# Four fused convolution layers: the order in which two engines empty the score tiles of layer 3, and the engine that normalises its input

## The chip, the cores and the metric

The kernel runs on one core of one Trainium2 chip. The metric is the device time of one execution in microseconds (us); lower is better. Five engines work side by side, each on its own queue of instructions in the order of the program: TensorE (in the profile PE for matmuls and PEld for its weight loads), VectorE (DVE), ScalarE (ACT), GpSimd (POOL) and SyncE (SP, which here only starts transfers). Matmuls write to PSUM, the accumulation memory; VectorE and ScalarE read it from there, GpSimd does not.

## The reference, cut to what matters

An input of 4 images, 256 channels, 48 x 48 points goes through four layers. Each adds its result to its input, and each starts by normalising the input in groups of 8 channels. Layer 3 is an attention whose sums run over square windows:

```python
def _gn(v, G=32, eps=1e-5):                 # group normalisation: (v - mean) / sqrt(var + eps)
    ...
def _L3_conv_ref(x, Wq, Wk, Wv, Wout, bout):        # WINDOWS = (1, 2, 4), HEADS = 8
    q = jax.nn.sigmoid(q)                   # q, k, v: projections of x, 8 heads of 32 channels
    k = jax.nn.sigmoid(k)
    v = v / jnp.maximum(jnp.linalg.norm(v, axis=1, keepdims=True), 1e-12)
    Ik = _integral(k)
    Ikv = _integral(jnp.einsum('bfhw,bghw->bfghw', k, v))
    for w in WINDOWS:
        ws = Hh // w                        # windows of 48, 24 and 12 points
        wk, wkv = _box(Ik, ws, Hh, Ww), _box(Ikv, ws, Hh, Ww)
        attn = jnp.einsum('bdhw,bdfhw->bfhw', q, wkv)
        norm = jnp.einsum('bdhw,bdhw->bhw', q, wk)
        outs.append((attn / (norm[:, None] + 1e-06)).reshape(b, C, Hh, Ww))
    return jnp.einsum('bchw,oc->bohw', jnp.concatenate(outs, axis=1), Wout) + bout[None, :, None, None]
...
x = x + _L3_conv_ref(_gn(x), L3_conv_Wq, L3_conv_Wk, L3_conv_Wv, L3_conv_Wout, L3_conv_bout)
```

For every query point this is: scores q.k against all key points, those outside the window set to zero, times v, for three windows.

## The kernel before

Layers 0 to 2 come first; towards their end the projections of the first image of layer 3 are woven in between them. The rest is the loop of layer 3. It walks over "tiles": one tile is a block of 128 keys (8 rows by 16 columns, block row `a`, block column `c` of 3) against a block of queries (8 rows, block row `rb`), for 4 heads. For the 4 images, two halves of the heads and six query blocks there are 720 tiles.

The four heads of a tile are two pairs. A pair's scores fill one PSUM tile `s` of two banks, one bank for each head, and there are two such tiles in all, so that the first pairs of all tiles share one and the second pairs the other:

```python
tc.tile_pool(name="smp", bufs=2 * (LAG + 1), reuse_waits="tile") as smp,      # LAG = 2
tc.tile_pool(name="ps_s", bufs=2, space=PSUM, reuse_waits="tile") as ps_s,
...
def scores(self, pr, a, c):
    s = ps_s.tile([P, 2, 512], F32, tag="s", name="s")
    for j in range(2):
        pe.matmul(s[:, j, ...], kvs[...][0][head, c, :], self.qs[head, r0:r1, c0:c1], start=True, stop=True)
```

Two engines empty `s` into the tiles `sm0`, `sm1`, `sm2` in SBUF, one for each window. `copy` (ScalarE) moves the columns on which the widest window has no edge, `widest` (VectorE) multiplies the columns beside them with a mask of zeros and ones, `middle` (VectorE) makes `sm1` by the mask of the middle window. GpSimd then makes `sm2` out of `sm0`:

```python
full = abs(a - rb) * RB + RB <= HALVES[0]      # all rows of the tile lie within the widest window
many = seen(NW - 1, a, rb)                     # the smallest window sees the tile: a "near" tile

def middle(s, tiles):
    if full and many:
        of_banks(s, tiles, 1, rows_seen(1, a, rb), cols_seen(1, c))       # dve.tensor_mul by mask 1
def copy(s, tiles):
    if full:
        act.copy(view(tiles, 0, (r0, r1), (f0, f1)), s[:, :, :, f0 - c0 : f1 - c0])
def widest(s, tiles):
    if not full:
        of_banks(s, tiles, 0, *all0)
        return
    for p0, p1 in ((c0, f0), (f1, c1)):
        if p0 < p1:
            of_banks(s, tiles, 0, (r0, r1), (p0, p1))                     # dve.tensor_mul by mask 0

first, second = zip(ss, pairs)
copy(*first)
middle(*second)
copy(*second)
middle(*first)
widest(*first)
widest(*second)
for tiles in pairs:
    wi = NW - 1 if many else 1
    if wi in wis:
        times_mask(pool, wi, ...)                                         # sm2 (or sm1) from sm0
```

TensorE runs two tiles behind with the sums: in one step it takes the scores of tile n, then the sums of tile n - 2 (`acc`, four heads for each window that sees the tile):

```python
for n in range(len(stream) + LAG):
    if n < len(stream):
        ss = [blocks[i].scores(pr, a, c) for pr in range(NPR)]
        ahead.append(blocks[i].masked(a, c, ss))
    if n >= LAG:
        sms = ahead.pop(0)
        for wi in (1, 0, 2):
            if wi in sms[0]:
                blocks[i].sums(wi, a, c, sms)
    advance()                      # one step of all jobs beside the loop: projections, norms, outputs
```

A query block alternates near tiles and the others ("far") as long as it has both. Tiles whose key rows are two blocks away are far but `full`; three blocks away they are not full, and VectorE empties them alone.

The projections of layer 3 take their input from `xn`, the normalised rows of x, made by VectorE with mean and reciprocal deviation from `st3`:

```python
xn = self.scr.tile([P, NCT, NKC, P], F32, tag="xn", name="xn")
for ct in range(NCT):
    dve.tensor_scalar(
        xn[:, ct].rearrange("p c (r x) -> p c r x", x=KC),
        xr[:, ct].rearrange("p r (c x) -> p c r x", x=KC),
        st3[:, b, 0, ct : ct + 1], st3[:, b, 1, ct : ct + 1], ALU.subtract, ALU.mult,
    )
    yield 1
...
# end of layer 2, once for each image
dve.tensor_copy(st3[:, b, 0, :], m3)
dve.tensor_copy(st3[:, b, 1, :], r3)
```

Of the kernel before, what the change touches and what calls it, by code (L numbers as in the profile page):

```python
# [15 lines left out]
AF = mybir.ActivationFunctionType  # L16
ALU = mybir.AluOpType
# [128 lines left out]
def conv_preact_kernel(  # L146
# [50 lines left out]
    st3 = const.tile([P, B, 2, NCT], F32, name="st3")  # L197


    pe, dve, act, pool, sync = (  # L200
        InOrder(tc, e) for e in (nc.tensor, nc.vector, nc.scalar, nc.gpsimd, nc.sync)
    )
# [69 lines left out]
    def take(what):  # L272
        while free[what] == 0:
            yield 1
        free[what] -= 1
# [11 lines left out]
    class Projection:  # L287
# [13 lines left out]
        def load(self, g, a, n):  # L301

            b = self.b
            yield from take("xr")
            if self.enough:
                free["xr"] += 1
                self.left.append(g)
                return
            xr = self.scr.tile([P, NCT, RB, W], F32, tag="xr", name="xr")
            sync.dma_start(  # L310
                out=xr,
                in_=x3_d[b][:, a * RB : (a + 1) * RB, :].rearrange(
                    "(ct p) r w -> p ct r w", p=P
                ),
            )
            yield FETCH
            yield from take("xn")
            xn = self.scr.tile([P, NCT, NKC, P], F32, tag="xn", name="xn")
            for ct in range(NCT):
                dve.tensor_scalar(  # L320
                    xn[:, ct].rearrange("p c (r x) -> p c r x", x=KC),
                    xr[:, ct].rearrange("p r (c x) -> p c r x", x=KC),
                    st3[:, b, 0, ct : ct + 1],
                    st3[:, b, 1, ct : ct + 1],
                    ALU.subtract,
                    ALU.mult,
                )
                yield 1
            free["xr"] += 1
            self.xn[g], self.uses[g] = xn, n  # L330
# [102 lines left out]
        def groups(self, groups):  # L433

            def load(n):
                a, names = groups[n]
                return self.load(n, a, sum(NKC if name == "v" else 1 for name in names))

            yield load(0)
            for n, (a, names) in enumerate(groups):
                if n + 1 < len(groups):
                    yield load(n + 1)
                for name in names:
                    if name == "v":
                        for c in range(NKC):
                            yield self.v(n, a, c)
                    else:
                        yield self.qk(n, a, name[0], int(name[1]))  # L450


    with (
# [766 lines left out]
        def layer2(b, stats):  # L1220
# [102 lines left out]
            late()  # L1323
            fill(1.5)
            m3, r3 = stats.end(fill)
            dve.tensor_copy(st3[:, b, 0, :], m3)
            dve.tensor_copy(st3[:, b, 1, :], r3)

        def prelude(b):
# [99 lines left out]
        with (  # L1429
# [11 lines left out]
            first = ExitStack()  # L1441
# [18 lines left out]
            for b in range(B):  # L1460
                if b + 1 < B:
                    filler = conv0(b + 1, {})
                else:
                    ending.close()
                    wts3 = ctx.enter_context(tc.tile_pool(name="wts_qkv", bufs=1, side="right"))
                    filler = project_first()
                    masks = wts3.tile([P, NMASK], BF16, name="masks")
                    nc.gpsimd.dma_start(out=masks, in_=masks_in[:, 0:NMASK])
                stats = attend(b)
                for _ in side:  # L1470
                    fill(1.5)
                load_wl1(0)
                load_wl1(1)
                load_wl2(0)
                layer2(b, layer1(b, stats))
                if b + 2 < B:
                    prelude(b + 2)
                else:
                    fill_all()
# [3 lines left out]
    with (  # L1483
# [187 lines left out]
        def rows_seen(wi, a, rb):  # L1671

            h = HALVES[wi]
            return (
                max(0, a * RB - h + 1 - rb * RB),
                min(RB, a * RB + RB + h - rb * RB),
            )

        def cols_seen(wi, c):
            h = HALVES[wi]  # L1680
            return max(0, c * KC - h + (wi > 0)), min(W, c * KC + KC + h)

        class Block:
# [28 lines left out]
            def masked(self, a, c, ss):  # L1712

                rb = self.rb
                all0 = rows_seen(0, a, rb), cols_seen(0, c)
                (r0, r1), (c0, c1) = all0
                wis = [wi for wi in range(NW) if seen(wi, a, rb)]
                pairs = [
                    {
                        wi: smp.tile(  # L1720
                            [P, 2, RB, min(W, KC + 2 * HALVES[wi])],
                            F32,
                            tag=f"sm{wi}",
                            name=f"sm{wi}",
                        )
                        for wi in wis
                    }
                    for _ in ss
                ]

                def view(tiles, wi, rows, cols):
                    (y0, _), (x0, _) = rows_seen(wi, a, rb), cols_seen(wi, c)
                    return tiles[wi][
                        :, :, rows[0] - y0 : rows[1] - y0, cols[0] - x0 : cols[1] - x0
                    ]

                def times_mask(engine, wi, rows, cols, dst, src):
                    mr = rb * RB + rows[0] - (a * RB - HALVES[wi] + 1)
                    mc = cols[0] - (c * KC - MCOL0[wi])
                    nr, ncol = rows[1] - rows[0], cols[1] - cols[0]  # L1740
                    m = mask[wi][:, mr : mr + nr, mc : mc + ncol]
                    engine.tensor_mul(
                        dst, src, m.unsqueeze(1).to_broadcast([P, 2, nr, ncol])
                    )

                def of_banks(s, tiles, wi, rows, cols):
                    src = s[:, :, rows[0] - r0 : rows[1] - r0, cols[0] - c0 : cols[1] - c0]
                    times_mask(dve, wi, rows, cols, view(tiles, wi, rows, cols), src)

                f0, f1 = max(0, c * KC + KC - HALVES[0]), min(W, c * KC + HALVES[0] + 1)
                full = abs(a - rb) * RB + RB <= HALVES[0]

                many = seen(NW - 1, a, rb)

                def middle(s, tiles):
                    if full and many:
                        of_banks(s, tiles, 1, rows_seen(1, a, rb), cols_seen(1, c))

                def copy(s, tiles):
                    if full:
                        act.copy(
                            view(tiles, 0, (r0, r1), (f0, f1)), s[:, :, :, f0 - c0 : f1 - c0]
# [8 lines that stand above are left out]
                            of_banks(s, tiles, 0, (r0, r1), (p0, p1))  # L1773

                first, second = zip(ss, pairs)
                copy(*first)
                middle(*second)
                copy(*second)  # L1780
                middle(*first)
                widest(*first)
                widest(*second)
                for tiles in pairs:

                    wi = NW - 1 if many else 1
                    if wi in wis:
                        rows, cols = rows_seen(wi, a, rb), cols_seen(wi, c)
                        src = view(tiles, 0, rows, cols)
                        times_mask(pool, wi, rows, cols, view(tiles, wi, rows, cols), src)  # L1790
                return [
                    {wi: view(t, wi, rows_seen(wi, a, rb), cols_seen(wi, c)) for wi in wis}
                    for t in pairs
                ]
# [28 lines left out]
        def seen(wi, a, rb):  # L1823
            r0, r1 = rows_seen(wi, a, rb)
            return r0 < r1
# [226 lines left out]
```

## Time and profile before

Three runs took 3774.7, 3778.4 and 3779.35 us, with a median of 3778.4 us. The profiled execution spans 3775.4 us.

| | whole span, 3775.4 us | loop of layer 3, 1440 to 3776 us |
|---|---|---|
| PE busy | 3264.8 | 2078.07 |
| PEld busy | 1879.4 | 941.82 |
| DVE busy | 2487.2 | 1543.65 |
| ACT busy | 1036.2 | 771.29 |
| POOL busy | 1518.1 | 1361.85 |

The first column is from the page's first part, the second is the sum of a table of busy time by stretch. The engines work side by side, so the rows don't add up. Matmuls overlap one another and their ends are modelled, so a busy PE isn't necessarily at its peak. Nearly every instruction is issued through one helper and carries its line number (L142); the groups are told apart by the names of their tiles, written out<-in: `sm<-s` empties a score tile, `acc<-sm,vs` are the sums. "idle before ... <-X" is the idle time of an engine just before such instructions, and what ended it.

### The profile page before, as it was taken

What the parts mean: (1) busy time and instruction counts of PE and PEld (TensorE: products, weight loads), DVE (VectorE), ACT (ScalarE), POOL (GpSimd) and SP (SyncE); (2) the same over time, 40 slices, a digit from 0 to 9 for tenths busy, and PEclk for the clock granted to TensorE, in tenths of its full rate; (3) what the DMA queues carried; (4) which work ended last, traced back from release to release, by engine and by line L of the source; (5) the groups of instructions that cost most, each with busy time, mean ns of one, the idle gap of its engine ahead of it and who ended that gap; (6) DMA issues with size and microseconds to landing.
All of it is one profiled execution on the core that took longest, in us unless ns stands there. A gap on an engine that the chain in (4) does not pass through costs nothing. (4 is left out here: it accounts for less than half of the span.)

```text
span 3775.4 us, 68847 instructions
## 1 busy us (share of the span) xinstructions
PE 3264.8 (86%) x26498; PEld 1879.4 (50%) x26498; DVE 2487.2 (66%) x5119; ACT 1036.2 (27%) x2025; POOL 1518.1 (40%) x2184
## 2 busy tenths in 40 slices
PE   3688898998996788988889889899899899989998
PEld 2467686786784564433334334344443344444443
DVE  7876587587583366777666567756577766556665
ACT  0012111111113322433222333332344332233331
POOL 0000120020020034778765486755365766344332
PEclk9798999999997899999999899999999999999999
DMA  7745323324324313345434243533223444101122
GB/s 250 238 135 170 100 104 116 109 95 125 109 75 124 102 70 108 125 136 159 125 103 131 90 136 122 164 97 108 78 95 123 139 116 116 47 31 53 41 60 60
DMA packets 373019, 423.04 MB, mean 112 GB/s; under 512 B 129076, under 2 KB 328532, under 8 KB 371540
## 3 DMA queue, kind: packets, MB, share of 16 engines
q1 hardware_dynamic: 371491, 416.32, 35.6%
q8 instruction: 211, 3.46, 0.4%
q0 software_dynamic: 144, 1.52, 0.2%
q14 instruction: 117, 0.95, 0.1%
q10 hardware_dynamic: 1056, 0.79, 0.1%
HBM read 288.79 MB, written 131.25 MB: 111 GB/s over the span
## 5 line engine op out<-in xcount | busy, mean ns | idle before, releaser
L142 DVE TENSOR_TENSOR sm<-s,masks 128x112 f32<-128x112 f32 (+10 forms) x2592 | 1135.8, 493 | 765.5 <-PE s L142 321.1
L142 POOL TENSOR_TENSOR sm<-sm,masks 128x432 f32<-128x432 f32 (+14 forms) x1152 | 853.3, 755 | 936.5 <-ACT sm L142 672.0
L142 PE MATMUL s<-qs,ks 32*128 32x320 f32 (+3 forms) x5760 | 832.5, 500 | 200.1 <-DVE sm L142 151.2
L142 ACT COPY sm<-s 128x528 f32<-128x528 f32 (+2 forms) x1152 | 594.9, 535 | 1470.7 <-PE s L142 1169.9
L142 PE MATMUL acc<-sm,vs 128*32 128x384 f32 (+18 forms) x13440 | 880.5, 385 | 16.1 <-POOL sm L142 15.8
L142 PEld LDWEIGHTS s<-qs,ks 32*128 32x128 f32 x5760 | 374.1, 185 | 604.7 <-DVE sm L142 232.8
L142 PE MATMUL cv<-vx,wt 128*128 128x288 f32 x2080 | 559.3, 425 | 90.7 <-DVE vx L142 49.1
L142 PEld LDWEIGHTS acc<-sm,vs 128*32 128x32 f32 x13440 | 355.2, 110 | 551.3 <-issue 348.6
L142 PEld LDWEIGHTS cv<-vx,wt 128*128 128x128 f32 x2080 | 402.4, 198 | 212.4 <-issue 53.6
L142 POOL MEMSET v<- 128x16 f32 (+1 forms) x120 | 18.6, 215 | 725.7 <-DVE vx L142 635.7
L142 PE MATMUL cv<-v,wl 128*128 128x384 f32 x1152 | 224.5, 354 | 24.4 <-DVE x L142 9.2
L142 PEld LDWEIGHTS cv<-v,wl 128*128 128x128 f32 x1152 | 214.8, 195 | 34.6 <-issue 16.1
L142 POOL TENSOR_TENSOR pt<-pt 128x144 f32<-128x144 f32 x336 | 187.4, 558 | 22.8 <-DVE pt L142 0.5
L142 POOL TENSOR_TENSOR v<-l2v,v 128x384 fp32r<-128x384 f32 x96 | 109.2, 1168 | 130.2 <-ACT v L142 121.4
L142 POOL TENSOR_TENSOR nhi<-nhi,nq 128x384 f32<-128x384 f32 x144 | 148.3, 1058 | 0.0
L142 PE MATMUL cv<-pad,wl 128*128 128x384 bf16 x864 | 143.1, 327 | 0.0
L142 PE MATMUL out_ps<-o,wout_sb 128*128 128x384 f32 x288 | 122.8, 509 | 9.4 <-DVE o L142 5.4
L142 PE MATMUL out_ps<-stage,wout_sb 128*128 128x384 f32 x288 | 117.3, 489 | 0.4 <-DVE stage L142 0.4
L142 PE MATMUL proj_ps<-wv_sb,xn 128*128 128x256 f32 x288 | 89.5, 438 | 32.3 <-ACT vt L142 19.1
L142 DVE TENSOR_TENSOR vx<-v 128x868 f32<-128x868 f32 x112 | 115.4, 1056 | 0.5
L142 PE MATMUL ap<-seen,xT 120*128 120x120 f32 (+3 forms) x832 | 113.5, 293 | 0.0
L142 PEld LDWEIGHTS <-wl 128*128 128x128 bf16 x864 | 83.8, 97 | 59.1 <-issue 0.4
(162 smaller groups left out, 2859.0 us busy)
## 6 DMA issues: line engine op xcount, KB each, us to landing
wt<-wt SPq DMA_DIRECT2D x48, 768.0 KB
kb_d<-pt SPq DMA_DIRECT2D x48, 576.0 KB
rc<-r_d SPq DMA_DIRECT2D x192, 144.0 KB
nhi<-kb_d SPq DMA_DIRECT2D x120, 192.0 KB
nlo<-kb_d SPq DMA_DIRECT2D x88, 192.0 KB
o_d<-stage SPq DMA_DIRECT2D x24, 576.0 KB
o<-o_d SPq DMA_DIRECT2D x24, 576.0 KB
wl<-wl_d SPq DMA_DIRECT2D x16, 768.0 KB
```

The source lines that it names most:

```text
L142: return lambda *args, **kwargs: self.tc.keep_in_program_order(op(*args, **kwargs))
```

## The change

For near tiles (`full and many`) the order is another: VectorE empties the first pair (`middle`, then `widest`) while ScalarE copies the second pair; then they change over, ScalarE copies the first pair and VectorE does the second. The other tiles keep their order. It is meant to let VectorE begin with the pair that is ready first, and to have each of the two score tiles emptied in one go. Separately the normalisation of the rows of x moves from VectorE to ScalarE, as an activation x * r + (-m * r); `st3` therefore holds -m * r in place of m.

```diff
@@ -317,13 +317,12 @@
             for ct in range(NCT):
-                dve.tensor_scalar(
+                act.activation(
                     xn[:, ct].rearrange("p c (r x) -> p c r x", x=KC),
                     xr[:, ct].rearrange("p r (c x) -> p c r x", x=KC),
-                    st3[:, b, 0, ct : ct + 1],
-                    st3[:, b, 1, ct : ct + 1],
-                    ALU.subtract,
-                    ALU.mult,
+                    AF.Identity,
+                    bias=st3[:, b, 0, ct : ct + 1],
+                    scale=st3[:, b, 1, ct : ct + 1],
                 )
                 yield 1
@@ -1323,7 +1322,7 @@
             m3, r3 = stats.end(fill)
-            dve.tensor_copy(st3[:, b, 0, :], m3)
+            dve.scalar_tensor_tensor(st3[:, b, 0, :], m3, -1.0, r3, ALU.mult, ALU.mult)
             dve.tensor_copy(st3[:, b, 1, :], r3)
@@ -1775,11 +1774,16 @@
                 first, second = zip(ss, pairs)
-                copy(*first)
-                middle(*second)
-                copy(*second)
-                middle(*first)
-                widest(*first)
+                if full and many:
+                    middle(*first)
+                    widest(*first)
+                    copy(*second)
+                    copy(*first)
+                    middle(*second)
+                else:
+                    copy(*first)
+                    copy(*second)
+                    widest(*first)
                 widest(*second)
                 for tiles in pairs:
```

## The prediction, made before the changed kernel was built or run

> **What bounds the kernel now.** I read the table of busy time by stretch first. The loop of layer 3 takes 1440 to 3776 us, 2336 us of the span, and its sum is
>
> ```profile
> sum 2336.00, PE 2078.07 PEld 941.82 DVE 1543.65 ACT 771.29 POOL 1361.85; mean PE 259.76 PEld 117.73 DVE 192.96 ACT 96.41 POOL 170.23
> ```
>
> PE is busy 2078 of 2336 us (89%), VectorE 66%, GpSimd 58%, ScalarE 33%. TensorE is the bound, and what an order of the other engines can win lies in the 258 us in which it idles. The waits in that stretch say for whom:
>
> ```profile
> DVE sm L142 <- PE s L142: 320.8, 341, 9.2
> ...
> PEld s L142 <- ACT sm L142: 164.9, 189, 2.1
> ```
> ```profile
> PE s L142 <- DVE sm L142: 151.2, 243, 3.9
> PE proj_ps L142 <- ACT sg L142: 18.3, 14, 6.1
> PE acc L142 <- POOL sm L142: 15.8, 17, 3.3
> ```
>
> (columns: us in total, times, the longest). 151 of the 258 us are TensorE waiting to write new scores into `s` until VectorE has let it go. Third, the timeline of one such wait, a near tile with `c` = 1:
>
> ```profile
> 3303.32 1.56 PE L142 MATMUL s<-qs,ks 32*128 32x384 f32 x8
> 3303.97 0.30 PEld L142 LDWEIGHTS s<-qs,ks 32*128 32x128 f32 x4 [0.35 <-DVE sm L142]
> 3304.34 0.61 ACT L142 COPY sm<-s 128x528 f32<-128x528 f32 x1 [3.12 <-PE s L142]
> ...
> 3304.81 1.33 PE L142 MATMUL acc<-sm,vs 128*32 128x216 f32 x24
> 3304.93 2.28 DVE L142 TENSOR_TENSOR sm<-s,masks 128x624 f32<-128x624 f32 x6 [1.02 <-PE s L142]
> ...
> 3305.83 0.62 ACT L142 COPY sm<-s 128x528 f32<-128x528 f32 x1 [0.88 <-POOL sm L142]
> ...
> 3306.95 0.71 PEld L142 LDWEIGHTS s<-qs,ks 32*128 32x128 f32 x8 [1.08 <-ACT sm L142]
> 3306.98 1.19 PE L142 MATMUL s<-qs,ks 32*128 32x320 f32 x8 [0.84 <-DVE sm L142]
> ```
>
> The first pair of scores is issued at 3303.32 and ScalarE starts on it at 3304.34; the second is issued 0.65 us later and VectorE starts on it at 3304.93. VectorE's six operations, start to start in the records, are `middle` second 0.72, `middle` first 0.72, `widest` first 0.20 + 0.18, `widest` second 0.20 and a last one of 0.27. The sums end at 3306.14, and TensorE idles 0.84 us until the first pair of the next tile may be written.
>
> **What the Trainium skill says.** "PSUM — Partial Sum Buffer", section on bank collisions: two engines must not access one bank and quadrant at once, two reads included, and software has to keep them apart. The trace agrees that they are kept apart: the copy of the second pair starts at 3305.83, after `middle` of the second (3304.93 + 0.81), although ScalarE was free from 3304.95. So each `s` is emptied by the two engines in turn, and the order in the program decides. "ScalarE: Activation LUTs", section on table sets: identity is in every set. The trace agrees as far as it goes: there are 68 table loads, and the existing identity activations (`pad<-x,off,gn_r`) follow a square root without one. The same page, section on the cost of a table load: a pointer operand for bias or scale adds some 93 ns to an activation; used below. "Perfetto Trace Analysis", section on the most-contended engine: a busy share of matmuls is a poor measure of how near TensorE is to its limit. I therefore count gaps only, and don't take 2078 us as a floor.
>
> **The reordering, on that tile.** Call the moment at which the first pair is ready 0 (3304.34), and g the time until the second is (here 0.61). Handing over between engines costs 0.06 to 0.1 us in these records.
> Before: the first `s` is free after g + 0.72 + 0.72 + 0.20 + 0.27 = 2.5; the second after two more `widest`, 2.9.
> After: VectorE takes the first pair from 0 to 1.2 (0.72 + 0.20 + 0.27); ScalarE copies the second from 0.61 to 1.23, then the first from 1.27 to 1.89. VectorE takes the second pair from about 1.3 to 2.45. The first `s` is free at 1.9, the second at 2.45.
> So the first comes 0.6 us earlier, the second 0.45.
>
> The gain comes from g: VectorE no longer waits for the second pair. If both pairs are ready together, as in
>
> ```profile
> 3313.95 0.93 PE L142 MATMUL s<-qs,ks 32*128 32x384 f32 x8
> ...
> 3314.97 0.62 ACT L142 COPY sm<-s 128x528 f32<-128x528 f32 x1 [2.55 <-PE s L142]
> 3314.97 2.28 DVE L142 TENSOR_TENSOR sm<-s,masks 128x624 f32<-128x624 f32 x6 [1.89 <-PE s L142]
> ```
>
> then the first `s` is free after 2 x 0.72 + 0.47 = 1.9 before, and after 1.2 + 0.06 + 0.62 = 1.9 in the new order: nothing is won. As the sums follow the second pair, I count the gain at the second `s`: g, but at most `middle` + `widest` - copy - 0.07, because the second copy must be done when VectorE comes to that pair. For `c` = 1 that cap is 1.11 - 0.62 - 0.07 = 0.42 us. For the outer columns `middle` is 0.53 start to start, `widest` 0.33, the copy 0.48 to 0.51: a cap of 0.30.
>
> **How often.** There are 384 near tiles (768 `middle` operations, two a tile). From the weight loads of `s`, eight a tile in order (5760 / 720), I took g and the TensorE gap ahead of the following tile:
>
> | near tiles | number | gap over 0.1 us | sum of gaps, us | mean g there | sum of min(gap, g, cap), us |
> |---|---|---|---|---|---|
> | c = 1 | 128 | 98 | 93 | 0.39 | 31 |
> | c = 0 | 128 | 31 | 17 | 0.45 | 6 |
> | c = 2 | 128 | 65 | 32 | 0.39 | 17 |
>
> Together 54 us (counted at the first `s` without the cap, 66). In the other 190 near tiles the sums last longer than the emptying, and nothing can be won. The remaining 58 us of gaps ahead of score matmuls follow far tiles, whose order stays.
>
> From the 54 I take off a fifth, 10 us, for tiles where VectorE or ScalarE is late with something else (projection evictions, table loads of 1.28 us, outputs), so that g isn't what holds.
>
> **GpSimd.** Its first `sm2` operation waits for the copy of the first pair, which moves from 0.6 us to 1.9 us after readiness; the second is then ready at once. It ends some 0.45 us later per near tile. The sums come two tiles later, about 6 us, so this mostly has slack; against the 15.8 us TensorE waits for it now I add 3 us.
>
> **The rows of x.** The records concerned:
>
> ```profile
> L142 DVE TENSOR_SCALAR xn<-xr,st x60: 643/665/673, 1161.4 to 2893.9; 128x384 f32<-128x384 f32 x60
> ```
> ```profile
> L142 ACT ACTIVATE sg<-proj_ps 128x384 f32<-128x384 f32 x96 | 47.6, 496 | 99.7 <-PE proj_ps L142 50.8 <-DMA q_d<-sg 48.1 <-ACT sg L142 0.4
> ...
> L142 ACT ACTIVATE pad<-x,off,gn_r 128x1152 f32<-128x1152 f32 x8 | 11.3, 1472 | 5.1 <-DVE off L142 5.1
> ```
>
> VectorE loses 60 x 0.665 = 40 us, 36 of the 60 inside the loop (24 us). ScalarE gains 60 operations. By the 0.496 us of an activation of that size without pointers plus two pointers I estimate 0.7 us each, 42 us. No table load is added. In the loop a 0.665 us block goes from the engine that lets `s` go to one that is idle two thirds of the time: some 36 x 0.2 = 7 us less waiting, an estimate (half of the tiles are near, half of those blocked, most of a block counts). The other 24 lie between 1161 and 1361 us, where ScalarE has many table loads and TensorE waits 53 us for `vt` and 39 for `sg`. There VectorE also stands 27 us in front of `xn` until the projection frees its buffer; that standing now moves to ScalarE, in front of other copies. I put a loss of 6 us there.
>
> **Sum:** -54 + 10 + 3 - 7 + 6 = -42. In addition what is won at the first `s` (66 in place of 54) counts where the sums aren't what follows closely; I take the middle, another -6. That makes -48: 3778 - 48 = 3730 us (-1.3%).
>
> **The rivals.**
> First, the wait moves rather than shrinks: ScalarE's copy of the first pair is now the last thing before `s` is free, so whatever holds ScalarE (1.26 us of three `stage` copies, table loads, the new `xn`) holds TensorE. For it: the wait of score weight loads for ScalarE's copies is listed with 165 us already. Against: ScalarE is 33% busy. It would halve the gain: 3750 us.
> Second, GpSimd becomes the bound: from 1440 to 2380 us it is busy 644 of 940 us, and its operations start later. That would give back up to 15 us in those stretches: 3740 us.
> Third, the gain is larger: if the tiles behind a near one also come free earlier and the 66 plus half of the gaps behind far tiles go, 66 + 29 = 95 less the 2 us of the rest: 3685 us.
> Fourth, the stretch around 1161 to 1361 us suffers: ScalarE standing 27 us in front of `xn` with the copies of layer 0 behind it, with half of the gain lost: 3750 us. The trace has nothing that excludes it.
>
> **Range and chances.** 3698 to 3758 us takes in the first two and fourth rivals, and most of the way to the third. Over 2% faster means under 3702.8, a gain of 76 us, more than all I count: 0.18. Slower by over 2% would need 76 us of new waits: 0.03. Within 2%: 0.79.
>
> **What would show it.** Right: PE waiting for VectorE at `s` falls from 151 to about 100 us, partly replaced by waiting for ScalarE at `s`; VectorE starts near tiles with the first pair and its wait for score matmuls falls; GpSimd's busy time stays; the 68 table loads stay; `xn` on ScalarE takes about 0.7 us. Wrong: the gaps behind near tiles stay at 141 us in sum, or PE's wait for `sm` of GpSimd grows by over 10 us, or the loop starts later than 1440 us by over 10.

## The result and the profile after

The changed kernel took 3739.11 us (median of 4, 3731.74 to 3740.3) against 3776.55 us for the kernel before on the same chip: a ratio of 0.9898, 95% interval 0.9881 to 0.9915, some 38 us. The prediction said 3730 us, 3698 to 3758.

The waits of TensorE in the loop of layer 3, changed kernel (us in total, times, the longest):

```profile
PE s L142 <- ACT sm L142: 65.2, 116, 3.4
PE s L142 <- DVE sm L142: 46.4, 97, 3.9
PE acc L142 <- POOL sm L142: 21.2, 23, 4.6
```

The wait for VectorE at the score tiles fell from 151 to 46 us. The wait for ScalarE, whose copy is now the last reader of the first score tile, rose from 14 to 65 us. Together 165 became 112. The wait for GpSimd rose by 5 us (15.8 before). VectorE's own wait for score matmuls fell from 321 to 214 us.

The tile of the prediction (the same keys, queries and image) in the timeline of the changed kernel:

```profile
3280.73 1.49 PE L142 MATMUL s<-qs,ks 32*128 32x384 f32 x8
3281.30 0.30 PEld L142 LDWEIGHTS s<-qs,ks 32*128 32x128 f32 x4 [0.28 <-DVE sm L142]
3281.69 2.49 DVE L142 TENSOR_TENSOR sm<-s,masks 128x624 f32<-128x624 f32 x6 [0.44 <-PE s L142]
...
3282.15 1.33 PE L142 MATMUL acc<-sm,vs 128*32 128x216 f32 x24
3282.34 1.24 ACT L142 COPY sm<-s 128x528 f32<-128x528 f32 x2 [3.63 <-PE s L142]
3283.63 0.30 PEld L142 LDWEIGHTS s<-qs,ks 32*128 32x128 f32 x4 [0.43 <-ACT sm L142]
3283.63 1.50 PE L142 MATMUL s<-qs,ks 32*128 32x320 f32 x8 [0.16 <-ACT sm L142]
3283.71 1.37 POOL L142 TENSOR_TENSOR sm<-sm,masks 128x270 f32<-128x270 f32 x2 [3.57 <-PE acc L142]
```

VectorE starts 0.96 us after the issue of the first pair (1.61 before) and ScalarE's two copies run back to back. The next tile's first pair is issued 2.90 us after this one's (3.63 before), and TensorE's gap is 0.16 us in place of 0.84. But look at the last matmul line: the next scores now take 1.50 us, not 1.19. Their two pairs come further apart (0.66 us, 0.38 before, from the first weight load of one pair to that of the other). GpSimd starts at 3283.71, after both copies.

The groups of score matmuls in the loop, first the kernel before, then the changed one (name, forms and count, then busy us, mean ns, and the idle time just before them):

```profile
L142 PE MATMUL s<-qs,ks 32*128 32x320 f32 (+1 forms) x5744 | 829.1, 499 | 194.4 <-DVE sm L142 151.2 <-ACT sm L142 13.7 <-ACT sg L142 8.7
```
```profile
L142 PE MATMUL s<-qs,ks 32*128 32x320 f32 (+1 forms) x5744 | 856.3, 498 | 121.2 <-ACT sm L142 65.2 <-DVE sm L142 47.5 <-DMA ks<-k_d 1.0
```

The idle time fell by 73 us, while the same matmuls, each as long as before (499 and 498 ns), kept TensorE busy for 27 us more. That is overlap that was lost: the records are as long as before, but fewer of them run at the same time.

The rows of x on ScalarE, by form:

```profile
L142 ACT ACT_TABLE_LOAD x68 | 87.2, 1283 | 2.3 <-PEq L2041 0.8 <-DMA q_d<-sg 0.4
L142 ACT ACTIVATE xn<-xr,st 128x384 f32<-128x384 f32 x60 | 41.1, 705 | 10.5 <-PE proj_ps L142 9.1 <-DMA xr<-x_d 1.4
```

Each takes 0.705 us (0.665 on VectorE), and the number of table loads is the 68 of before.

From the first score to the end, the loop took 2345.9 us before and 2313.8 us after. In this pair of profiles the loop also starts 13 us earlier, but 7.6 us of that are there before the first row of x is normalised, and a second profile of the changed kernel starts its loop at 1430.2 us, the kernel before at 1429.5. I therefore count only the 32 us; in that second profile it is 26 (2319.7 us).

### The profile page after: what moved, and what is told of

Read it like the earlier page. It is cut to its first block, busy times and chain, and to the rows that moved or that the text cites. A ratio compares the mean times of both kernels' runs of the same rounds, so it can differ in the third digit from the quotient of the medians.

```text
span 3730.0 us, 69121 instructions
## 1 busy us (share of the span) xinstructions
PE 3284.1 (88%) x26498; PEld 1873.8 (50%) x26498; DVE 2494.9 (67%) x5059; ACT 1067.4 (29%) x2085; POOL 1528.0 (41%) x2184
## 5 line engine op out<-in xcount | busy, mean ns | idle before, releaser
L142 DVE TENSOR_TENSOR sm<-s,masks 128x112 f32<-128x112 f32 (+10 forms) x2592 | 1149.2, 492 | 704.7 <-ACT sm L142 297.1
L142 POOL TENSOR_TENSOR sm<-sm,masks 128x432 f32<-128x432 f32 (+14 forms) x1152 | 883.1, 788 | 900.9 <-ACT sm L142 397.5
L142 PE MATMUL s<-qs,ks 32*128 32x320 f32 (+3 forms) x5760 | 859.7, 499 | 127.8 <-ACT sm L142 65.2
L142 PEld LDWEIGHTS cv<-v,wl 128*128 128x128 f32 x1152 | 212.7, 193 | 34.0 <-issue 15.8
L142 DVE TENSOR_TENSOR pt<-cs 128x384 f32<-128x384 f32 x144 | 119.2, 827 | 0.0
```

What stands on the lines that cost most here:

```text
L142: return lambda *args, **kwargs: self.tc.keep_in_program_order(op(*args, **kwargs))
```

## The experiments

Below, "the gaps behind near tiles" are the idle time of TensorE ahead of the score matmuls of the tile that follows a near tile, all 384 in sum; they are measured ahead of its first pair. A near tile is called blocked if that gap was over 0.1 us in the kernel before. Ratios are to the kernel before on the same chip, with a 95% interval.

The theory: TensorE waits behind near tiles for the score tiles; the new order frees the second one earlier by g (the time between the two pairs becoming ready) up to a cap. Rivals: the relief of VectorE by the rows of x; the first score tile alone governs; a start with the ready pair is what counts; GpSimd takes part of it back.

**The order alone.**

```diff
 # the kernel before, with the new order of near tiles; rows of x on VectorE
```

> The new order of the near tiles alone; the rows of x stay on VectorE. My theory (the gain lies in the score tiles of near tiles coming free earlier, the move of the rows is worth next to nothing): 3735 to 3750 us, at least three quarters of the gain of the whole change (37 us), and the gaps of TensorE behind near tiles fall from 141 us to 70 to 90. Rival (the relief of VectorE by the rows of x brings most of it): 3760 us or more.

Measured: 3751.82 us against 3785.76, ratio 0.9914 (0.9892 to 0.9936). The gaps behind near tiles are 74 us (141 before, 73 in the changed kernel). The time is just outside my range, which was set for a kernel before of 3778 us; the gain, 33 us by the ratio, is inside what I expected. The group of score matmuls looks much as in the changed kernel (this view holds all 5760 records, those above 5744):

```profile
L142 PE MATMUL s<-qs,ks 32*128 32x320 f32 (+3 forms) x5760 | 864.6, 503 | 134.4 <-ACT sm L142 64.9 <-DVE sm L142 54.5 <-DMA ks<-k_d 7.3
```

The order carries most of the gain.

**The rows alone.**

```diff
-                dve.tensor_scalar(xn..., st3[..0..], st3[..1..], ALU.subtract, ALU.mult)
+                act.activation(xn..., AF.Identity, bias=st3[..0..], scale=st3[..1..])
 # and st3 as in the change; the old order of near tiles
```

> The rows of x on ScalarE alone; the old order of the near tiles. My theory: 3768 to 3782 us, within 0.25% of the kernel before, with about -7 us in the loop of layer 3 and -6 to +6 us in the stretch from 1150 to 1430 us. Rival (the relief of VectorE brings most): 3750 us or less.

Measured: 3783.04 us, ratio 0.9992 (0.9978 to 1.0006). The gaps behind near tiles stay at 140 us, and so does the group of score matmuls, but for 9 us less idle time:

```profile
L142 PE MATMUL s<-qs,ks 32*128 32x320 f32 (+1 forms) x5742 | 829.1, 500 | 185.2 <-DVE sm L142 142.5 <-ACT sm L142 13.2 <-ACT sg L142 8.7
```

The rival falls: 40 us less work on VectorE are worth 3 us by this run, with an interval of 8 us gained to 2 us lost.

**First or second score tile?**

```diff
                 copy(*first)
-                middle(*second)
                 copy(*second)
                 middle(*first)
                 widest(*first)
+                middle(*second)
                 widest(*second)
```

> Rows of x on VectorE; in near tiles ScalarE copies both pairs first, and VectorE then does all of the first pair, then all of the second. By the sums of the prediction (c = 1, from readiness of the first pair, g = 0.61): the first score tile free at 0.68 + 1.2 = 1.9 as in the changed kernel (2.5 before), the second only at 3.05 (2.9 before, 2.45 changed). If the second tile governs, as the prediction counts: no gain, 3770 to 3790 us. If the first tile governs: about the gain of the new order alone, 3740 to 3750 us. Between: both count.

Measured: 3806.89 us, ratio 1.0058 (1.004 to 1.0076), slower by 22 us. That is outside both ranges. Its gaps behind near tiles are 74 us ahead of the first pair, as low as with the new order, and yet it loses. The timeline of the same tile shows how:

```profile
3331.00 1.26 PE L142 MATMUL s<-qs,ks 32*128 32x384 f32 x8
3331.96 1.12 ACT L142 COPY sm<-s 128x528 f32<-128x528 f32 x2 [3.82 <-PE s L142]
...
3332.61 2.28 DVE L142 TENSOR_TENSOR sm<-s,masks 128x624 f32<-128x624 f32 x6 [1.31 <-ACT sm L142]
...
3333.95 0.81 PE L142 MATMUL s<-qs,ks 32*128 32x320 f32 x4 [0.42 <-DVE sm L142]
...
3335.01 0.33 PEld L142 LDWEIGHTS s<-qs,ks 32*128 32x128 f32 x4 [0.77 <-issue]
3335.04 0.81 PE L142 MATMUL s<-qs,ks 32*128 32x320 f32 x4 [0.28 <-DVE sm L142]
```

The next first pair comes after 2.91 us, as early as in the changed kernel, but the second only 1.10 us later (0.66 there), with a gap of its own of 0.28 us. Such gaps ahead of second pairs are another 27 us behind near tiles in this run; the kernel before and the changed one have none there. Each pair then runs alone for 0.81 us, and the sums behind them wait. In the group of score matmuls of this run the busy time went up:

```profile
L142 PE MATMUL s<-qs,ks 32*128 32x320 f32 (+1 forms) x5744 | 925.0, 504 | 147.7 <-DVE sm L142 124.2 <-issue 6.2 <-ACT vt L142 4.2
```

96 us more than before, against 47 us less idle time. Only about 8 of the 96 come from longer matmuls (504 ns against 499). So a first score tile that comes free earlier brings no gain when the second comes later, and gaps alone don't show it. The size of the loss is less sure than its sign: in the 19 executions of the kernel before on this chip, 0.001 less of the clock granted to TensorE went with some 2.7 us more, and these six ran at 0.946 against 0.949 on average, which would be 8 of the 22 us by that estimate.

**A start with the ready pair, the two widest last.** First without a limit to near tiles, which also turned round the copies of the far tiles:

```diff
+                middle(*first)
+                copy(*second)
                 copy(*first)
                 middle(*second)
-                copy(*second)
-                middle(*first)
                 widest(*first)
                 widest(*second)
```

> Rows of x on VectorE; VectorE begins with middle of the first pair while ScalarE copies the second, then they change over, but the two widest come last as before. By the same sums: middle first ends at 0.72, middle second waits for the copy until 1.3 and ends at 2.0, widest first at 2.5, widest second at 2.95, so neither tile comes earlier than before (2.5 and 2.9). Theory that starting with the ready pair is enough: gain as in the new order alone, 3740 to 3750 us. My theory (the time at which the tiles come free counts): 3770 to 3790 us.

Measured: 3923.31 us, ratio 1.0368 (1.0343 to 1.0392). I had expected no change and had overlooked the far tiles: behind those two blocks away the gaps rose from 31 to 128 us. The same again with `if full and many`, the other tiles as in the changed kernel:

> As the interleaved order, but for near tiles alone; the far tiles copy the first pair first, as before. In the run without that limit the far tiles copied the second pair first as well, and TensorE's gaps behind the tiles two blocks away rose from 31 to 128 us. My theory (starting with the ready pair brings nothing if the two widest still come last; the loss of the earlier run was the far tiles'): 3780 to 3805 us, at 0.999 to 1.005 of the kernel before. Rival (the interleaving itself cost the 3.7%): 3850 us or more.

Measured: 3808.73 us, ratio 1.0065 (1.0041 to 1.0088), gaps behind tiles two blocks away 33 us, behind near tiles 156 us. A start with the ready pair brings nothing while the widest come last. It is just slower than my range: behind the outer columns the second pair of the following tile comes 0.11 to 0.13 us later (median of the blocked tiles). The difference between the two runs is 3%, some 115 us; between their profiles it is 97 us (3907.8 and 3811.0). Of these, 83 us lie at the 192 far tiles of two blocks away (from their second pair to the following one), 0.43 us for each tile in which ScalarE copied the second pair ahead of the first.

**Only the middle columns.**

```diff
-                if full and many:
+                if full and many and c == 1:
 # else: the old order; rows of x on VectorE
```

> Rows of x on VectorE; the new order only for near tiles with c = 1, the old one for the outer columns. The sums of the prediction put 31 of 54 us on c = 1; the new order in all near tiles has meanwhile measured 0.86% (some 32 us). My theory (the gain is set by g and the caps, so it divides 31 to 23): 0.992 to 0.997 of the kernel before, near 0.995 (18 us). Rival (the gain comes from GpSimd or from the rhythm of the whole loop, not from single tiles): nothing of it below 0.999, or all of it at 0.9915.

Measured: 3759.44 us, ratio 0.9931 (0.9909 to 0.9953), 26 us by the ratio and 23 between the medians. That is in my range, but the interval also takes in 0.9915, so the time alone doesn't exclude that all of the gain is here. The profile divides it: the gaps behind near tiles with `c` = 1 fell from 93 to 51 us, as in the changed kernel, while those behind `c` = 2 and `c` = 0 stayed at 31 and 17 us (12.5 and 9 in the changed kernel). `c` = 1 carries more than its share of 31 in 54; one reason is that the new order brings next to nothing in the column `c` = 0, as the next run and the sums further down show.

**GpSimd's order.** In a few tiles with `c` = 0 that were not blocked, the changed kernel is slower by 1 to 3 us each. One of them, from the timeline of the changed kernel:

```profile
2233.65 1.38 PE L142 MATMUL acc<-sm,vs 128*32 128x312 f32 x16
...
2235.02 2.06 POOL L142 TENSOR_TENSOR sm<-sm,masks 128x324 f32<-128x324 f32 x2
2235.88 0.14 PEld L142 LDWEIGHTS acc<-sm,vs 128*32 128x32 f32 x4 [1.55 <-POOL sm L142]
2235.88 0.47 PE L142 MATMUL acc<-sm,vs 128*32 128x162 f32 x4 [0.85 <-POOL sm L142]
2237.04 2.89 POOL L142 TENSOR_TENSOR nhi<-nhi,nlo 128x384 f32<-128x384 f32 x3
2237.13 0.14 PEld L142 LDWEIGHTS acc<-sm,vs 128*32 128x32 f32 x4 [1.10 <-POOL sm L142]
2237.13 0.47 PE L142 MATMUL acc<-sm,vs 128*32 128x162 f32 x4 [0.78 <-POOL sm L142]
```

TensorE has the sums of two windows done and waits twice for `sm2`, which GpSimd makes late, behind its work on the norms (`nhi`). GpSimd takes the first pair first, whose copy now comes last. So I let it take the second pair first:

```diff
-                for tiles in pairs:
+                for tiles in reversed(pairs) if full and many else pairs:
```

> The changed kernel, but GpSimd makes sm2 of the second pair ahead of that of the first in near tiles, since its copy now comes first. If GpSimd's later start cost the some 9 us by which a few near tiles are slower (sums held up by sm2): 3 to 9 us faster than the changed kernel, 0.9875 to 0.989 of the kernel before. Rival (the sums come two tiles later anyway and it has slack): no difference, 0.9895 to 0.991.

Measured: 3733.31 us, ratio 0.9865 (0.9839 to 0.9891). That is more than I expected. Four of those tiles are longer by 1.4 to 3.3 us in both profiles of the changed kernel (counted from the issue of their second pair to that of the following second pair). Three of them are back or nearly so: 7.58, 5.51 and 8.13 us became 4.91, 3.87 and 6.50 (4.26, 3.87 and 6.50 in the kernel before). The fourth stays at 6.92 (5.51 before). As the two versions had run on different chips, both once more on one:

> The changed kernel itself, to stand beside the version with GpSimd's other order on one chip: 0.988 to 0.9915 of the kernel before. If the earlier difference between the two (0.9898 and 0.9865, on different chips) came from the chips, both lie within 0.1% of each other here.

Measured: 3740.49 us (3729.02 to 3751.67), ratio 0.9896 (0.9876 to 0.9917).

> The changed kernel with GpSimd taking the second pair first in near tiles, again, on the same chip as the changed kernel. If GpSimd's order costs what the single tiles show (the loop of layer 3 was 8.6 us shorter in the profile, three slow tiles back at their old length): 4 to 10 us less than the changed kernel. Rival: less than 3 us apart.

Measured: 3724.74 us (3721.5 to 3733.54), ratio 0.9856 (0.9834 to 0.9878). It is 16 us ahead of the changed kernel on the same chip, more than the 4 to 10 expected; the intervals of the two ratios overlap by a hair, but it is ahead in both comparisons. The same tile in this version:

```profile
2238.80 1.59 POOL L142 TENSOR_TENSOR sm<-sm,masks 128x324 f32<-128x324 f32 x2
2240.35 3.38 POOL L142 TENSOR_TENSOR nhi<-nhi,nlo 128x384 f32<-128x384 f32 x3
2240.44 0.16 PEld L142 LDWEIGHTS acc<-sm,vs 128*32 128x32 f32 x8 [1.45 <-POOL sm L142]
2240.44 0.48 PE L142 MATMUL acc<-sm,vs 128*32 128x162 f32 x8 [0.75 <-POOL sm L142]
```

One wait in place of two. This is the fastest version of the study.

## Why the prediction was right, and what was mis-sized

**The bound and the mechanism** held for two of the three columns. The gain is behind near tiles, it is counted at the second score tile, and for `c` = 1 and `c` = 2 g with its cap sets it where g is not small. For the blocked tiles, the time from the issue of their first pair to that of the following second pair fell, from the records of the changed kernel, by (medians, in us):

| | g near 0.11 | g near 0.4 | g near 0.65 |
|---|---|---|---|
| c = 1: predicted, measured | 0.11, 0.06 (23 tiles) | 0.38, 0.38 (50) | 0.42, 0.37 (25) |
| c = 2: predicted, measured | 0.11, 0.00 (17) | 0.30, 0.29 (33) | 0.30, 0.27 (15) |
| c = 0: predicted, measured | 0.11, 0.00 (7) | 0.30, -0.13 (13) | 0.30, 0.29 (11) |

In the middle of the last row the tiles became longer by this count. Counted from their second pair they are 0.17 us shorter: their own first pair is now issued 0.29 us further ahead of the second. A second profile of the changed kernel gives the same medians within 0.01 us.

**The term of 54 us** was too big. Counted from second pair to second pair, these tiles shrank by 22.7 us for `c` = 1 (31 predicted), 10.0 for `c` = 2 (17) and 3.8 for `c` = 0 (6): 36.5 us. The discount of 10 us for other work on the engines would have given 44. Two things are missing in it: tiles with small g bring nothing, or half of g (see the table), and in some tiles the median is reached but not the mean (0.14 us for `c` = 2 with g near 0.65).

**The addition of 6 us** for what is won at the first score tile was wrong in kind. Gaps behind near tiles fell by 69 us, more than I counted, but score matmuls with less overlap took 27 us back. The copies-first run shows it at its barest: the same gaps ahead of the first pairs, and a loss.

**GpSimd** was predicted at 3 us. TensorE's wait for it at the sums grew by 5 us, and three tiles with `c` = 0 became longer by 6.6 us together and recover when GpSimd's order is turned round. So the second rival was right in its mechanism and my term was too small. All near tiles with `c` = 0 that were not blocked became longer by 11.7 us, but not all of that is the new order's: in the rows-alone run the same tiles are 8.1 us longer, at other places than these three. What else the turned order wins, to make 16 us, is not settled: in the two profiles of that chip the loop differs by 19 us, spread over many tiles, most of it (13.7 us) at far tiles. GpSimd's busy time, which I had said would stay, went from 1518 to 1528 us, and is 1517 with its order turned round.

**The rows of x** came out as predicted: 0.705 us each for an estimate of 0.7, no table load more, and a sum (-7 + 6) next to nothing, which the rows-alone run gives as 3 us with an interval that includes zero. Neither part shows. From the first row of x to the start of the loop there are 262 to 270 us in six profiles with the rows on VectorE and 262 to 267 us in five with them on ScalarE; so the loss of 6 us, and with it the fourth rival, was not seen. The 53 and 39 us on which I had based it also add up waits of weight loads and of matmuls that run at the same time; TensorE itself stood for 24 and 16 us. The loop of the rows-alone run takes 2348.0 us (2345.9 before), with no gain of 7 us to be seen; two profiles of one kernel differ by 6.

**The sum** came out closer than its parts: some 38 us of the 48 predicted. From second pair to second pair, the loop of the changed kernel is shorter by 36.5 us at blocked tiles, longer by 9.9 at the other near tiles, and shorter by 6.0 at far tiles, for which I had counted nothing: 32.6 us. In its second profile the far tiles give only 2.5. My statement that 76 us is more than all I count was not right either, as the third rival counts 93; nothing of it came, the gaps behind far tiles only went from 58 to 55 us.

**The first rival,** ScalarE as the new last reader, shows in the waits (65 us at `s`), perhaps only as the place where the remaining wait is booked; that it costs anything by ScalarE being late with other work was not tried.

## What to carry to other kernels

When two engines empty two accumulation tiles in turn, work out when each tile comes free and count at the one the next work needs last; here an early start on the first, or freeing the first alone, brought nothing. Let an engine begin with what is ready first and finish it in one go. Then try the consumers behind it in the new order as well; here using first what is copied first brought another 0.4% (0.9896 to 0.9856). Idle gaps of TensorE are not a gain in hand, because a gap can turn into matmuls that no longer overlap.

## What the runs showed of the hardware that I had not expected

Two pairs of these small matmuls (32 rows each; the profile has eight records for the four heads of a tile) overlap when they are issued together: the eight take 0.93 us, and 1.56 us when the second pair comes 0.65 us later. So lateness of a second pair costs TensorE time that counts as busy: 829 us of score matmuls in the loop became 925 us in the copies-first run, with the same matmuls of about 500 ns each. The ends of matmuls are modelled in the profile; that time was really lost shows in the loop, 2381.8 us in that run against 2345.9.
